# A low-bit test of the square weights, moved from the last units to the kernel's first microseconds

## The chip, the cores and the metric

The kernel runs on one core of a Trainium2 chip. A core has a matrix engine (TensorE, PE in the profile; its weight loads are listed as PEld), a vector engine (VectorE, DVE), a scalar engine (ScalarE, ACT), a general engine (GpSimd, POOL) and a queue processor (SyncE, SP). Each engine works through its own instructions in the order in which they were written, and waits on semaphores for the others. SyncE and ScalarE issue the transfers (DMA); SPq and ACTq are these issues in the profile. Data lies in HBM, in the on-chip memory SBUF (128 partitions), and in PSUM, where TensorE writes. The metric is device time in microseconds, from runs of the whole kernel.

## What is computed

The input x is 8 sequences of 512 positions with 128 features, in float32. A stack of six attention layers runs on the layer norm of x, and its result is added to x. A ternary feed-forward block runs on the layer norm of that, and is added again. Cut to what matters:

```python
def layer(h, p):                                   # six times
    q = (h @ wq.T + bq).reshape(bh, sl, 16, 8)
    k = (h @ wk.T + bk).reshape(bh, sl, 16, 8)
    scores = einsum('blhd,bmhd->bhlm', q, k) / sqrt(8)
    w_avg = softmax(scores).mean(axis=1)           # mean over 16 heads
    new_w = softmax(w_avg + rel)                   # rel: decay with distance
    h1 = ln(h + new_w @ h);  h2 = ln(h1)
    ff = relu(h2 @ w1.T + b1) @ w2.T + b2
    return ln(h2 + ff)

x = x + stack(layernorm(x))
v = layernorm(x)
h = silu((v @ w1.T) * s1) * ((v @ w2.T) * s2)      # 128 -> 512, weights -1, 0, 1
h = gelu((h @ h1.T) * t1);  h = gelu((h @ h2.T) * t2)   # 512 -> 512
x = x + (h @ w3.T) * s3
```

## The kernel before

**Units and steps.** A unit is one layer for one sequence: 6 x 8 = 48 units, layer by layer (`units`, line 222). A unit has 32 steps (`PAIRS`). A step makes two score tiles of 128 rows by 512 keys: 32 query positions for four heads in one matmul (line 451). For each tile VectorE takes the negated row maximum (`top`, line 462) and ScalarE the exponential with its row sum (`e`, line 471). A group is two steps; eight steps make one block of 128 positions (`lc`), and four blocks a unit.

**Stacks.** The score matmuls run on stacked operands. `project_k` and `project_q` multiply the transposed input hT by the layer's `wqk`; ScalarE writes kT and qT with their biases (lines 257 and 266, the biases from `bk_col` and from `bqs`, which VectorE scales out of `bq_col` in line 710). VectorE cuts each into a high part with the low twelve bits cleared (`hik`, `hiq`, line 274), GpSimd forms the remainder (`lok`, `loq`, line 275) and spreads the query parts under a head mask (`m0`, `m1`, line 311). Transfers then stack them: `stack_k` (16 of them into `ks`), `stack_q` (16 for half a unit into `qs`). In the first unit `stack_first` builds the first half in 32 smaller ones, and ScalarE issues a part of these and of `stack_k`. The pool for `qs` has two buffers. Two of the first unit's masks stand in buffers of the `e` pool, which are needed again for its third group.

**The order of the work** is written by hand. `at(step, place, fn)` puts a piece of work at a place within a step; steps are counted from the first unit's start, those before it from -64 on. In the prologue the first sequence's norm stands at steps -55 to -35, the transpose of its result at -33, `bqs` at -32, its projections at -28 and -27, `split_k` at -26, `split_q` at -24, the masks and `stack_first` at -14 and -13. The second sequence's norm stands at -12 to -3. `plan_before` and `plan_after` place a unit's preparation and its end (norms, MLP) into the steps of its neighbours; `sum_rows`, a GpSimd addition of two rows of the layer's parameters, is at step 3 of a layer's first unit. Between the engines the order of issue of the transfers is found by the program's builder, and each transfer signals its end on one of a few semaphores, which are used in turn.

**Loads at the start.** SyncE loads x of sequences 0 and 1 (256 KB each), then `load_layer(0)`: wqk (128 KB), w1, w2 (256 KB each) and `rows` (448 KB: seven parameter rows, copied to all partitions). ScalarE issues nine small loads of columns (line 125), behind three activations over the decay table and ahead of its copy of hT (line 250). In the code, the column loads stand between the loads of x and `load_layer(0)`. Later layers are loaded in the same order from unit 4 of the layer before.

**The low-bit test.** The block at the end has two arms. `gated_split` uses a faster matmul form that asks for weights whose low twelve bits are zero; `gated` is the general one. To choose, the kernel looks at the ten square weight blocks (fw1, fw2, and four blocks each of fh1 and fh2, 128 x 512): `load_square(k)` brings a block from HBM into a staging tile `square` (pool tag `x`) and copies it from there to its place; `low_bits(k)` keeps the low bits with an AND on VectorE (line 157) and takes their maximum (line 160). This is spread over units 41 to 45, two blocks a unit, the loads at steps 1 and 16, the tests at 7 and 23. `low_bits_row` reduces the ten maxima to one column (line 164) and sends it by a transfer into one row, in the last unit's step 7; `low_bits_end` reduces the row (line 168) in step 23. After the last unit, all engines read the number and take one arm (line 939).

Of the kernel before, what the change touches and what calls it, by code (L numbers as in the profile page):

```python
# [9 lines left out]
F32 = mybir.dt.float32  # L10
F32R = mybir.dt.float32r
I32 = mybir.dt.int32
# [5 lines left out]
P = 128  # L18
# [11 lines left out]
def attn_stack_then_ffn(ctx: ExitStack, tc: tile.TileContext, a: dict, out: bass.AP):  # L30
# [65 lines left out]
        nc.sync.dma_start(t, x[b].rearrange("(c p) e -> p c e", p=P))  # L96
        return t

    for b in range(2):
        x_in[b] = load_x(b, f"in{b}")  # L100
    lay = {}

    def load_layer(d):
        qk = wts.tile([P, 2, E], F32, tag="wqk", name=f"wqk_{d}", bufs=2)
        nc.sync.dma_start(qk, a["wqk"][d].rearrange("t e o -> e t o"))
        w1 = wts.tile([P, F], F32, tag="w1", name=f"w1_{d}", bufs=2)
        nc.sync.dma_start(w1, a["w1t"][d])
        w2 = wts.tile([P, FC, E], F32, tag="w2", name=f"w2_{d}", bufs=2)
        nc.sync.dma_start(w2, a["w2t"][d].rearrange("(c p) e -> p c e", p=P))
        r = wts.tile([P, len(ROWS), E], F32, tag="rows", name=f"rows_{d}", bufs=2)  # L110
        nc.sync.dma_start(
            r.rearrange("p k e -> p (k e)"),
            a["rows"][d].rearrange("k e -> (k e)").partition_broadcast(P),
        )
        rows = {name: r[:, k, :] for k, name in enumerate(ROWS)}
        lay[d] = (qk, w1, w2, rows)

    cols = {}
    for name, shape in (
# [3 lines left out]
    ):  # L123
        cols[name] = wts.tile(shape, F32, tag=name, name=name)
        nc.scalar.dma_start(cols[name], a[name])
    load_layer(0)

    fw1 = wts.tile([P, HID], F32, name="fw1")
    fw2 = wts.tile([P, HID], F32, name="fw2")
    fh1 = wts.tile([P, HC, HID], F32, name="fh1")  # L130
# [8 lines left out]
    low = state.tile([P, 2 + 2 * HC], I32, name="low")  # L139
    low_row = state.tile([1, P], I32, name="low_row")  # L140
    low_any = state.tile([1, 1], I32, name="low_any")

    staged = {}

    def load_square(k):

        name, c = ("f_w1t", "f_w2t", "f_h1t", "f_h2t")[k if k < 2 else 2 + (k - 2) // HC], (k - 2) % HC
        t = staged[k] = state.tile([P, HID], F32, tag="x", name=f"square_{k}", bufs=3)
        nc.sync.dma_start(t, a[name] if k < 2 else a[name][c * P : (c + 1) * P, :])
        nc.sync.dma_start(  # L150
            (fw1, fw2)[k] if k < 2 else (fh1, fh2)[(k - 2) // HC][:, c, :], t
        )

    def low_bits(k):

        t = staged.pop(k)
        nc.vector.tensor_scalar(
            t.bitcast(I32), t.bitcast(I32), ~LOW12, None, ALU.bitwise_and
        )
        nc.vector.tensor_reduce(low[:, k : k + 1], t.bitcast(I32), AX.X, ALU.max)  # L160

    def low_bits_row():
        most = state.tile([P, 1], I32, name="low_most")
# [3 lines left out]
    def low_bits_end():  # L167
        nc.vector.tensor_reduce(low_any, low_row, AX.X, ALU.max)

    bqs = wts.tile([P, D], F32, name="bqs")  # L170


# [60 lines left out]
    class Unit:  # L233
# [18 lines left out]
        def project_k(self):  # L252
            d = self.d
            pk = ring([P, L], f"pk_{self.n}")
            self.kT = work.tile([P, L], F32, tag="kT", name=f"kT_{self.n}", bufs=1)
            nc.tensor.matmul(pk, lay[d][0][:, 1, :], self.hT, start=True, stop=True)
            return lambda: nc.scalar.activation(  # L257
                self.kT, pk, AF.Identity, bias=cols["bk_col"][:, d : d + 1]
            )

        def project_q(self):
            d = self.d
            pq = ring([P, L], f"pq_{self.n}")
            self.qT = work.tile([P, L], F32, tag="qT", name=f"qT_{self.n}", bufs=1)
            nc.tensor.matmul(pq, lay[d][0][:, 0, :], self.hT, start=True, stop=True)
# [79 lines left out]

        def sum_rows(self):

            rows = lay[self.d][3]
# [4 lines left out]
            self.ln = Norm(self.z1, self.z1, f"a{self.n}")  # L353

        def affine_a(self, k):
            rows = lay[self.d][3]
# [7 lines left out]
            self.ln = Norm(self.z1, self.v, f"b{self.n}")  # L364

        def affine_b(self, k):
            rows = lay[self.d][3]
# [13 lines left out]
            )  # L381

        def hidden(self, f):
            w1 = lay[self.d][1]
            if f == 0:
                self.g = work.tile([P, FC, L], F32, tag="g", name=f"g_{self.n}", bufs=1)
            pf = ring([P, L], f"pf_{self.n}_{f}")
            nc.tensor.matmul(pf, w1[:, f * P : (f + 1) * P], self.uT, start=True, stop=True)  # L388
            k = self.d * FC + f
            def relu():  # L390
                if f == 1:
                    nc.vector.tensor_scalar(
                        self.g[:, f, :], pf, cols["b1_col"][:, k : k + 1], 0.0, ALU.add, ALU.max
                    )
                else:
                    nc.scalar.activation(
                        self.g[:, f, :], pf, AF.Relu, bias=cols["b1_col"][:, k : k + 1]
                    )

            return relu  # L400

        def mlp_out(self, half):
            w2 = lay[self.d][2]
# [14 lines left out]
            self.ln = Norm(self.z3, self.z3, f"c{self.n}")  # L418

        def affine_c(self, k):  # L420
            rows = lay[self.d][3]
# [281 lines left out]
    def plan_before(un):  # L703

        t = un.u * PAIRS
        if un.d == 0:
            first_steps = (20, 21, 26, 28, 29) if un.u == 1 else (9, 14, 26, 28, 29)
            norm_steps(t - 2 * PAIRS, un, un.norm_in, *first_steps)
        if un.u == 0:
            at(-PAIRS, D2, lambda: nc.vector.tensor_scalar_mul(bqs, cols["bq_col"], ISD))  # L710
        s = t - PAIRS
        matmuls(s, (5, P1, 5, A0), un.project_k)
        matmuls(s, (4, P0, 5, A1), un.project_q)
        at(s + 6, D2, un.split_k)
# [298 lines left out]
```

## Time and profile before

| | |
|---|---|
| median of three runs | 2647.22 us (2646.22 to 2648.22) |
| profiled execution, its own time | 2649.35 us |
| its span in the profile | 2647.4 us |
| granted TensorE clock over the span | 0.994 |
| first exponential of the first unit (ACT, line 471) | at 26.8 us |
| one unit in the middle of the kernel | 49.6 us |
| line 392, one instruction a unit: its 38th and its 45th start | 1989.28 and 2348.18 us |
| DMA traffic | 273.66 MB, of which 13.86 MB read from HBM |

All times in the profile count from the span's start and come from one execution; the times of runs are of executions without a profile. A line of the groups gives line, engine, operation, output and inputs, count and durations; a line of the timeline gives start, duration, engine and line; a line of the chain gives start, duration and what the end of the kernel waited for then. "Landing" is the time from the issue of a transfer to its completion.

### The profile page before, as it was taken

To read this page: it belongs to the slowest core of one execution; us is meant where nothing else is said; L and a number is where in the kernel's file an instruction comes from. 1 tells how busy PE (TensorE), PEld (TensorE's weight loads), DVE (VectorE), ACT (ScalarE), POOL (GpSimd) and SP (SyncE) were. 2 spreads that over 40 slices of the span, in tenths; PEclk is the share of its full clock that TensorE was granted. 3 is DMA by queue.
4 is the path that set the end of the run, shared out by engine and by line. 5 is a ranking of instruction groups with operands and counts; after the bars stand their busy time and mean duration, and the time that the engine had idled before them with its cause. 6 is when DMAs were issued, how large, how long until landed. Compare 5 with 4: busy or idle time off the path is not lost.

```text
span 2647.4 us, 50361 instructions
## 1 busy us (share of the span) xinstructions
PE 2559.2 (97%) x14944; PEld 1437.8 (54%) x14944; DVE 2489.0 (94%) x5773; ACT 2459.8 (93%) x6798; POOL 1812.5 (68%) x1894
## 2 busy tenths in 40 slices
PE   6999999999999999999999999999999999998999
PEld 2455555555555555555555555555555555555787
DVE  5999999999999999999999999999999999998774
ACT  6999999999999999999999999999999999997443
POOL 4667777677677677677677677677677667675874
PEclk8999999999999999999999999999999999999999
DMA  6445444455444444444445454455444545541000
GB/s 144 107 115 124 104 113 103 104 114 119 105 112 103 105 113 120 105 114 102 105 111 122 104 114 102 104 114 120 104 112 110 127 119 122 130 95 41 9 25 17
DMA packets 135846, 273.66 MB, mean 103 GB/s; under 512 B 39696, under 2 KB 57232, under 8 KB 135568
## 3 DMA queue, kind: packets, MB, share of 16 engines
q1 hardware_dynamic: 133504, 269.31, 43.8%
q8 instruction: 121, 1.98, 0.3%
q10 hardware_dynamic: 2064, 1.08, 0.2%
q14 instruction: 157, 1.29, 0.2%
HBM read 13.86 MB, written 2.10 MB: 6 GB/s over the span
## 4 chain that ended last, share of the span: by engine, by line
ACT 36%; DVE 32%; PE 26%; issue 3%; POOL 1%; DMA 1%; SPq 1%; ACTq 0%; POOLq 0%; DVEq 0%
ACT e L471 31%; DVE top L462 24%; PE acc L493 9%; PE ps L451 6%; PE qh L579 4%; DVE wT L511 2%; PE po L519 1%; PE pf L388 1%; ACT w L501 1%; ACT uT L378 1%; DVE z L415 1%; PE fo L625 1%; ACT kT L257 1%; PE pt_w L213 1%; PE q L579 1%
## 5 line engine op out<-in xcount | busy, mean ns | idle before, releaser
L471 ACT ACTIVATE e<-ps,top 128x512 f32<-128x512 f32 x3072 | 2092.5, 735 | 54.7 <-DVE top L462 29.2
L462 DVE TENSOR_REDUCE top<-ps 128x1 f32<-128x512 f32 x3072 | 1921.2, 679 | 60.5 <-PE ps L451 54.4
L451 PE MATMUL ps<-ks,qs 128*128 128x512 f32 x3040 | 1155.8, 469 | 27.7 <-ACT e L471 19.5
L451 PEld LDWEIGHTS ps<-ks,qs 128*128 128x128 f32 x3040 | 531.7, 188 | 666.0 <-ACT e L471 419.8
L471 ACT ACTIVATION_READ_ACCUMULATOR e<-ps,top 128x1 f32 x3072 | 780.6, 254 | 0.0
L493 PE MATMUL acc<-e,rp 128*32 128x512 f32 x6144 | 740.4, 600 | 0.8 <-POOL rp L482 0.8
L493 PEld LDWEIGHTS acc<-e,rp 128*32 128x32 f32 x6144 | 160.4, 109 | 331.2 <-issue 328.0
L482 POOL TENSOR_TENSOR rp<-pick,r 128x256 f32<-128x256 f32 x384 | 237.4, 618 | 133.8 <-DVE r L480 93.4
L311 POOL TENSOR_TENSOR m<-hiq,mask 128x512 f32<-128x512 f32 x190 | 242.2, 1286 | 0.7 <-DMA qs_first<-m_first 0.7
L311 POOL TENSOR_TENSOR m<-loq,mask 128x512 f32<-128x512 f32 x190 | 241.4, 1283 | 0.0
L519 PEld LDWEIGHTS po<-h,wT 128*128 128x128 f32 x1536 | 202.0, 192 | 17.3
L519 PE MATMUL po<-h,wT 128*128 128x129 f32 x1536 | 203.3, 275 | 0.0
L388 PE MATMUL pf<-uT,w 128*128 128x512 f32 x384 | 196.6, 593 | 3.7 <-ACT e L471 1.7
L408 PEld LDWEIGHTS py<-w,g 128*128 128x128 f32 x1536 | 182.6, 191 | 23.4 <-ACT e L471 19.1
L408 PE MATMUL py<-w,g 128*128 128x128 f32 x1536 | 191.7, 278 | 0.0
L197 POOL TENSOR_TENSOR rs_c<-mv_c,eps 128x4 f32<-128x4 f32 x48 | 9.7, 202 | 248.0 <-DVE r L480 228.3
L213 PE MATMUL pt_w<-ident,w 128*128 128x128 f32 x768 | 120.8, 280 | 17.7 <-ACT e L471 7.8
L275 POOL TENSOR_TENSOR lok<-kT,hik 128x512 f32<-128x512 f32 x48 | 61.5, 1280 | 101.6 <-DVE hik L274 101.6
L511 DVE TENSOR_TENSOR wT<-pt_w,decay 128x512 f32<-128x512 f32 x192 | 129.8, 676 | 0.1
L501 ACT ACTIVATE w<-acc 128x512 f32<-128x512 f32 x192 | 123.2, 642 | 0.0
L213 PEld LDWEIGHTS pt_w<-ident,w 128*128 128x128 f32 x768 | 86.4, 141 | 59.0 <-ACT e L471 45.2
L275 POOL TENSOR_TENSOR loq<-qT,hiq 128x512 f32<-128x512 f32 x48 | 61.4, 1279 | 76.6 <-DVE hiq L274 76.6
(116 smaller groups left out, 2665.8 us busy)
## 6 DMA issues: line engine op xcount, KB each, us to landing
qs<-m SPq DMA_DIRECT2D x1520, 128.0 KB, 2.4
ks<-hik SPq DMA_DIRECT2D x384, 64.0 KB, 2.0
ks<-lok SPq DMA_DIRECT2D x376, 64.0 KB, 2.0
rows<-in_rows SPq DMA_DIRECT2D x6, 448.0 KB, 5.1
x_in<-in_x SPq DMA_DIRECT2D x8, 256.0 KB, 3.0
fh<-square SPq DMA_DIRECT2D x8, 256.0 KB, 2.3
x_out<-in_x SPq DMA_DIRECT2D x8, 256.0 KB, 2.9
out<-y SPq DMA_DIRECT2D x7, 256.0 KB, 2.4
```

The source lines that it names most:

```text
L213: nc.tensor.transpose(pt[:, c * P : (c + 1) * P], src[:, c, :], ident)
L311: nc.gpsimd.tensor_tensor(m[:, lc - 2 * two], part.unsqueeze(2).to_broadcast([P, NB, PER_STRIP, QB]), mask.unsqueeze(1).to_broadcast([P, N ...
L388: nc.tensor.matmul(pf, w1[:, f * P : (f + 1) * P], self.uT, start=True, stop=True)
L408: nc.tensor.matmul(self.py[:, k, :], self.g[:, f, c * P : (c + 1) * P], w2[:, f, :], start=(f == 0), stop=(f == FC - 1),)
L451: nc.tensor.matmul(ps[s], qs[:, nb * P : (nb + 1) * P].bitcast(F32R), un.ks[:, i, :].bitcast(F32R), start=True, stop=True,)
L462: nc.vector.tensor_reduce(top[s], ps[s], AX.X, ALU.max, negate=True)
L471: nc.scalar.activation(self.e[:, nb, :], ps[s], AF.Exp, bias=top[s], accum_out=self.zs[:, i % 2, nb : nb + 1],)
L482: nc.gpsimd.tensor_tensor(self.rp.rearrange("p t n l -> p (t n) l"), pick.unsqueeze(1).to_broadcast([P, 2 * NB, QB]), r.rearrange("p t n - ...
L493: nc.tensor.matmul(acc[nb * QB : (nb + 1) * QB, :], self.rp[:, gr.turn % 2, nb, :], gr.e[:, nb, :], start=(gr.turn == 0), stop=(gr.turn == ...
L501: nc.scalar.activation(self.w.rearrange("p c l -> p (c l)"), acc, AF.Exp, scale=1.0 / H)
L511: nc.vector.tensor_tensor(self.wT.rearrange("p c l -> p (c l)"), self.pt, decay[:, LC - 1 - lc : 2 * LC - 1 - lc, :].rearrange("p c l -> p ...
L519: nc.tensor.matmul(self.po, self.wT[:, c, :], self.unit.h[:, c, 0 : E + 1], start=(c == 0), stop=(c == LC - 1),)
```

## The change

`load_layer` is split. `load_qk(d)` loads wqk alone; for layer 0 it stands between the loads of the two first sequences. The rest of layer 0 (w1, w2, rows) is loaded at the beginning of unit 0's loop body, on SyncE behind the stacks of the first half unit and the load of sequence 2. `sum_rows` of the first unit moves from step 3 to step 12.

`look_at_square` loads all ten square blocks from HBM at the start, behind x of sequence 1, two blocks to a part: the first part into the buffer of tag `g` (the MLP's hidden tile, first needed for the first unit in unit 2), the other four into one buffer of tag `qs` (16 KB a partition), which is the one that the first unit's second half takes. `low_bits(part)` now tests two blocks, 1024 columns, with the same two instructions: parts 0 and 1 at steps -31 and -30, parts 2, 3 and 4 at step -5, `low_bits_row` at step -4 and `low_bits_end` at the second unit's first step. `load_square` stays where it was, with both of its transfers, and no test follows it.

```diff
-    for b in range(2):
-        x_in[b] = load_x(b, f"in{b}")
+    def load_qk(d):
+        lay_qk[d] = wts.tile([P, 2, E], F32, tag="wqk", name=f"wqk_{d}", bufs=2)
+        nc.sync.dma_start(lay_qk[d], a["wqk"][d].rearrange("t e o -> e t o"))
...
     def load_layer(d):
-        qk = wts.tile([P, 2, E], F32, tag="wqk", name=f"wqk_{d}", bufs=2)
-        nc.sync.dma_start(qk, a["wqk"][d].rearrange("t e o -> e t o"))
...
+    x_in[0] = load_x(0, "in0")
+    load_qk(0)
+    x_in[1] = load_x(1, "in1")
...
-    load_layer(0)
...
+    def look_at_square():
+
+        first = work.tile([P, 2, HID], F32, tag="g", name="look_first", bufs=1)
+        rest = proj.tile([P, 2 * HC, HID], F32, tag="qs", name="look_rest")
+        for part in range(1 + HC):
+            looked[part] = first if part == 0 else rest[:, 2 * part - 2 : 2 * part, :]
+            for k in range(2):
+                nc.sync.dma_start(looked[part][:, k, :], square_block(2 * part + k)[0])
 
     def load_square(k):
 
-        name, c = ("f_w1t", "f_w2t", "f_h1t", "f_h2t")[k if k < 2 else 2 + (k - 2) // HC], (k - 2) % HC
-        t = staged[k] = state.tile([P, HID], F32, tag="x", name=f"square_{k}", bufs=3)
-        nc.sync.dma_start(t, a[name] if k < 2 else a[name][c * P : (c + 1) * P, :])
...
-    def low_bits(k):
-
-        t = staged.pop(k)
-        nc.vector.tensor_scalar(
-            t.bitcast(I32), t.bitcast(I32), ~LOW12, None, ALU.bitwise_and
-        )
-        nc.vector.tensor_reduce(low[:, k : k + 1], t.bitcast(I32), AX.X, ALU.max)
+        src, dst = square_block(k)
+        t = state.tile([P, HID], F32, tag="x", name=f"square_{k}", bufs=3)
+        nc.sync.dma_start(t, src)
+        nc.sync.dma_start(dst, t)
+
+    def low_bits(part):
+
+        t = looked.pop(part).bitcast(I32)
+        nc.vector.tensor_scalar(t, t, ~LOW12, None, ALU.bitwise_and)
+        nc.vector.tensor_reduce(low[:, part : part + 1], t, AX.XY, ALU.max)
...
+    look_at_square()
     bqs = wts.tile([P, D], F32, name="bqs")
...
-            at(t + 3, D2, un.sum_rows)
+            at(t + (12 if un.u == 0 else 3), D2, un.sum_rows)
...
+    for k, step in enumerate((-31, -30, -5, -5, -5)):
+        at(step, D2, lambda k=k: low_bits(k))
+    at(-4, D2, low_bits_row)
+    at(PAIRS, D2, low_bits_end)
...
-        at((U - 7 + k // 2) * PAIRS + (7, 23)[k % 2], D2, lambda k=k: low_bits(k))
-    at((U - 1) * PAIRS + 7, D2, low_bits_row)
-    at((U - 1) * PAIRS + 23, D2, low_bits_end)
...
         if un.b == 4 and un.d + 1 < D:
+            load_qk(un.d + 1)
             load_layer(un.d + 1)
+        if u == 0:
+            load_layer(0)
```

More of the change, by code (lines that the diff above doesn't have):

```diff
@@ L97, in load_x @@
         return t
-    for b in range(2):
-        x_in[b] = load_x(b, f"in{b}")
-    lay = {}
+    lay_qk, lay = {}, {}
+    def load_qk(d):
+        lay_qk[d] = wts.tile([P, 2, E], F32, tag="wqk", name=f"wqk_{d}", bufs=2)
+        nc.sync.dma_start(lay_qk[d], a["wqk"][d].rearrange("t e o -> e t o"))
     def load_layer(d):
-        qk = wts.tile([P, 2, E], F32, tag="wqk", name=f"wqk_{d}", bufs=2)
-        nc.sync.dma_start(qk, a["wqk"][d].rearrange("t e o -> e t o"))
         w1 = wts.tile([P, F], F32, tag="w1", name=f"w1_{d}", bufs=2)
@@ L114, in load_layer @@
         )
-        rows = {name: r[:, k, :] for k, name in enumerate(ROWS)}
-        lay[d] = (qk, w1, w2, rows)
+        lay[d] = w1, w2, {name: r[:, k, :] for k, name in enumerate(ROWS)}
+    x_in[0] = load_x(0, "in0")
+    load_qk(0)
+    x_in[1] = load_x(1, "in1")
     cols = {}
@@ L137, in load_ffn, with square_block @@
         nc.sync.dma_start(fw3s, a["f_w3s"].partition_broadcast(P))
-    low = state.tile([P, 2 + 2 * HC], I32, name="low")
+    low = state.tile([P, 1 + HC], I32, name="low")
     low_row = state.tile([1, P], I32, name="low_row")
     low_any = state.tile([1, 1], I32, name="low_any")
-    staged = {}
-    def load_square(k):
-        name, c = ("f_w1t", "f_w2t", "f_h1t", "f_h2t")[k if k < 2 else 2 + (k - 2) // HC], (k - 2) % HC
-        t = staged[k] = state.tile([P, HID], F32, tag="x", name=f"square_{k}", bufs=3)
-        nc.sync.dma_start(t, a[name] if k < 2 else a[name][c * P : (c + 1) * P, :])
-        nc.sync.dma_start(
-            (fw1, fw2)[k] if k < 2 else (fh1, fh2)[(k - 2) // HC][:, c, :], t
-        )
-    def low_bits(k):
-        t = staged.pop(k)
-        nc.vector.tensor_scalar(
-            t.bitcast(I32), t.bitcast(I32), ~LOW12, None, ALU.bitwise_and
-        )
-        nc.vector.tensor_reduce(low[:, k : k + 1], t.bitcast(I32), AX.X, ALU.max)
+    looked = {}
+    def square_block(k):
+        if k < 2:
+            return a[("f_w1t", "f_w2t")[k]], (fw1, fw2)[k]
+        c = (k - 2) % HC
+        name, t = (("f_h1t", fh1), ("f_h2t", fh2))[(k - 2) // HC]
+        return a[name][c * P : (c + 1) * P, :], t[:, c, :]
+    def look_at_square():
[5 more added lines that the diff above has]
+                nc.sync.dma_start(looked[part][:, k, :], square_block(2 * part + k)[0])
+    def load_square(k):
+        src, dst = square_block(k)
[6 more added lines that the diff above has]
+        nc.vector.tensor_reduce(low[:, part : part + 1], t, AX.XY, ALU.max)
     def low_bits_row():
@@ L255, in project_k @@
             self.kT = work.tile([P, L], F32, tag="kT", name=f"kT_{self.n}", bufs=1)
-            nc.tensor.matmul(pk, lay[d][0][:, 1, :], self.hT, start=True, stop=True)
+            nc.tensor.matmul(pk, lay_qk[d][:, 1, :], self.hT, start=True, stop=True)
             return lambda: nc.scalar.activation(
@@ L264, in project_q @@
             self.qT = work.tile([P, L], F32, tag="qT", name=f"qT_{self.n}", bufs=1)
-            nc.tensor.matmul(pq, lay[d][0][:, 0, :], self.hT, start=True, stop=True)
+            nc.tensor.matmul(pq, lay_qk[d][:, 0, :], self.hT, start=True, stop=True)
             return lambda: nc.scalar.activation(
@@ L346, in sum_rows @@
         def sum_rows(self):
-            rows = lay[self.d][3]
+            rows = lay[self.d][2]
             rows["b2s"] = wts.tile([P, E], F32, tag="b2s", name=f"b2s_{self.d}", bufs=2)
@@ L355, in affine_a @@
         def affine_a(self, k):
-            rows = lay[self.d][3]
+            rows = lay[self.d][2]
             if k == 0:
@@ L366, in affine_b @@
         def affine_b(self, k):
-            rows = lay[self.d][3]
+            rows = lay[self.d][2]
             if k == 0:
@@ L383, in hidden @@
         def hidden(self, f):
-            w1 = lay[self.d][1]
+            w1 = lay[self.d][0]
             if f == 0:
@@ L402, in mlp_out @@
         def mlp_out(self, half):
-            w2 = lay[self.d][2]
+            w2 = lay[self.d][1]
             self.py = ring([P, 2, E], f"py_{self.n}_{half}")
@@ L420, in affine_c @@
         def affine_c(self, k):
-            rows = lay[self.d][3]
+            rows = lay[self.d][2]
             if k == 0:
```

## The prediction

> **What bounds the kernel now.** I read the page first, then the groups of one tile, a timeline of VectorE (DVE), busy times by window, and last the chain of waits at the kernel's start. The page's first part:
>
> ```profile
> PE 2559.2 (97%) x14944; PEld 1437.8 (54%) x14944; DVE 2489.0 (94%) x5773; ACT 2459.8 (93%) x6798; POOL 1812.5 (68%) x1894
> ```
>
> Three engines above 90%: whatever keeps one of them may show one for one. The tile that stages a square weight block has these VectorE groups (duration minimum, median, maximum in ns; first and last start in us):
>
> ```profile
> L157 DVE TENSOR_SCALAR square<-square x10: 417/470/535, 2078.2 to 2312.0; 128x512 int32<-128x512 int32 x10
> L160 DVE TENSOR_REDUCE low<-square x10: 685/686/689, 2078.7 to 2312.5; 128x1 int32<-128x512 int32 x10
> ```
>
> They occupy 10 x (0.470 + 0.686) = 11.56 us of VectorE between 2078 and 2313. What that costs is read off an instruction that runs once a unit, the VectorE relu of line 392, in the timeline (start, duration):
>
> ```profile
> 1989.28 0.74 DVE L392 TENSOR_SCALAR g<-pf,b_col 128x512 f32<-128x512 f32 x1
> ...
> 2038.89 0.75 DVE L392 TENSOR_SCALAR g<-pf,b_col 128x512 f32<-128x512 f32 x1
> ...
> 2348.18 0.74 DVE L392 TENSOR_SCALAR g<-pf,b_col 128x512 f32<-128x512 f32 x1
> ```
>
> A clean unit takes 2038.89 - 1989.28 = 49.61 us. The next six, which hold all ten tests, take 309.29 us, or 11.6 more than six clean ones. Busy times of a clean window and of one unit with two tests (window, length; PE, PEld, DVE, ACT, POOL; clock, DMA share, GB/s):
>
> ```profile
> 1000.00:1050.00 50.00, 49.34 (x300) 26.66 (x292) 48.88 (x115) 49.53 (x142) 34.98 (x37) 1.00 0.53 128
> 2141.50:2193.60 52.10, 50.54 (x294) 26.73 (x293) 50.71 (x119) 49.53 (x140) 34.62 (x37) 1.00 0.51 124
> ```
>
> The reader should see ACT: 0.47 us idle in the first window, 2.57 in the second. ScalarE bounds the clean unit; during a test it runs out of row maxima. So the tests stand on the path in full. Now the start, by the chain of waits:
>
> ```profile
> 3.32 5.36 DMA rows<-in_rows
> 8.69 0.33 ACTq L125
> 9.07 0.45 ACTq L125
> 9.55 0.59 ACT hT L250
> 10.19 2.07 PE pq L265 x2
> 12.27 1.47 PE pk L256 x2
> 13.76 0.70 ACT kT L257
> 14.48 0.44 DVE hik L274
> ...
> 33.85 2.04 DMA qs_first<-m_first
> 36.07 0.63 ACT e L471
> ```
>
> The first copy on ScalarE, hT, stands behind ScalarE's nine column loads, and the last two of these were held by the landing of `rows`. The issues just before show the rule, beside the landing times of SyncE's last loads (us from issue, last column):
>
> ```profile
> 6.73 0.33 ACTq L125 DMA_DIRECT2D f_w1s_col<-in_f_w1s_col  x1
> 7.56 0.33 ACTq L125 DMA_DIRECT2D f_w2s_col<-in_f_w2s_col  x1
> ```
>
> ```profile
> rows<-in_rows SPq DMA_DIRECT2D x1, 448.0 KB, 5.4
> w<-in_w1t SPq DMA_DIRECT2D x1, 256.0 KB, 4.4
> w<-in_w2t SPq DMA_DIRECT2D x1, 256.0 KB, 4.7
> ```
>
> w1, issued at 2.32, lands at 6.72; w2, issued at 2.84, at 7.54; rows, issued at 3.32, at 8.69. At just these moments f_w1s, f_w2s and f_h1s go out. Counting issues (SyncE's six: x0, x1, wqk, w1, w2, rows; then ScalarE's nine), w1 is fourth and f_w1s twelfth: an issue waits until the transfer eight places earlier has landed.
>
> **The change, part by part.**
>
> *Tests leave the units* (`low_bits` at steps 7 and 23): ten pairs go, -11.6 us by the six units. The other measure, VectorE's busy time, gives 11.56; I take 11.6, with 10 as the lower end, should the `load_square` waits on SyncE, which stay, carry some of it. `low_bits_row` (one 0.15 us reduction) leaves unit U-1 too, -0.15; `low_bits_end` (0.26 us) only changes its unit, 0.
>
> *Ten loads of 256 KB enter SyncE's queue at the start; w1, w2, rows leave it.* Ahead of both groups stand the same 640 KB (x0, x1, wqk in another order), so the first square load should land where w1 did, at 6.7 us. From w1's landing to that of rows, 704 KB took 1.97 us, 366 GB/s; each further 256 KB adds 0.72 us, and the tenth lands at 6.7 + 9 x 0.72 = 13.2. By w2's gap alone (0.82 us per 256 KB) it is 14.1, by that of rows (1.15 us per 448 KB) 12.6. SyncE itself takes about 0.5 us an issue, thirteen by 8 us; its last two wait for the first square loads, at 6.7 and 7.4 us, with over 1 MB still under way, so nothing runs dry.
>
> *What waits for them.* By the count above, f_h1s becomes the twenty-first issue and waits for the thirteenth, the tenth square load; f_h2s waits for bq, the fourteenth. Behind them on ScalarE's queue stand hT, kT, qT and half of the stack copies; PE's pq waits for hT, VectorE's hik for kT, both stack queues for hik. From rows' landing to hT it was 0.86 us; now 13.2 + 0.86 = 14.1 against 9.55: **+4.5 us** (3.9 to 5.4). PE's transposes for hT end at 9.35, so the whole delay shows. From hik to the e of 36.07 the chain is queue issues and their landing, and from 36 to 85 us ScalarE is busy 47.64 of 49.00: the delay reaches the end one for one.
>
> *Two tests in front of hik* (steps -31, -30, behind bqs). bq landed at 8.86, 0.17 after rows, though issued at 4.18; I take 0.17 after the tenth load, 13.4. A test now covers 1024 columns, at most twice the old pair, 2.3 us, and not under 1.8 if a quarter of it is fixed cost. They end at 17.2 to 18.2; hik is due at 14.48 + 4.5 = 19.0. Cost 0, hidden by the two projections on PE; without that cover up to 4.6.
>
> *Three tests at step -5*, behind unit 1's statistics, which end at 17.6 + 4.5 = 22.1: 5.4 to 6.9 us, and longer beside POOL's masks (hiq took 1.47 us beside POOL's lok, hik 0.43 alone: up to 1.04 more for each). They end at 27.5 to 32.1; the first row maximum is due at 25.39 + 4.5 = 29.9. Up to 2.2 late, covered by the 3.33 us that ScalarE idles before 36.07 for an e buffer. POOL may lose a VectorE operation (at most 1.07) now and then: ScalarE's queue takes the second mask 1.4 us after it is ready and SyncE its third about 5 after, so 0 to 0.7; I take 0. If both covers went: up to 2.9.
>
> *SyncE in unit 0.* The low_row issue (0.54), w1, w2 and rows (0.47, 0.43, 0.50) now precede sixteen stack copies: 1.9 us later, and 960 KB at 366 GB/s are 2.7 us of transfer. The thirteenth copy (issued near 44.0, landing 2.4 to 2.9 later) completes the first strip that the matmul at 52.08 reads; 5.2 us of cover against 4.6. Cost 0, at worst 1. `sum_rows` at step 12 lies on POOL between the rp at 43.01 and that at 49.94; rows should be in at about 43.3, all on the old clock. The looked-at buffers: the g slot is first used in unit 2, the stack slot at 36, both after the tests.
>
> *Sum*: -11.6 - 0.15 + 4.5 = -7.3 us. The profiled execution took 2649.35 (span 2647.4 and 1.95 around it), so it would take 2642.1; it stands 2.13 above the median of the runs, 2647.22, from which I forecast **2639.9 us**.
>
> One rule speaks against the change. The Trainium skill, "DMA: Bandwidth & Descriptors", section "Anatomy of one DMA", gives each DMA about 2.0 us plus its bytes over 436 GB/s (fitted on another issue path). Taken one after another, ten loads of 256 KB would be an estimated 26 us against 8 for the three that leave, and the sum +6. The rows above speak for overlap, landing 0.8 and 1.15 us apart.
>
> **Rivals.**
>
> *A, column loads not behind the square loads.* If the order of issues puts ScalarE's nine ahead of most square loads, hT stays near 9.6. For it: on ScalarE they are ready at 4.18, when SyncE has issued some seven loads. Against it: before, all six loads of SyncE were counted first, though four stand behind the columns in the code. Time: 2647.2 - 11.75 = 2635.5.
>
> *B, a later start.* The tests show in front of hik (bqs more than 1 us late), or the bulk runs at 200 GB/s rather than 366: 1600 KB more at the head cost 8.2 us instead of 4.5. For it: the slowest 0.3 us of the old burst moved 176 GB/s. Against: w1, w2 and rows. Time: 2647.2 - 11.75 + 8.5 = 2644.
>
> *C, slower: the loads run one after another.* A square load alone took 2.9 us to land; ten in series are 29 us, less the three removed in the same way (2.9 + 2.9 + 5.1): +18.1 at hT, 2653.6. It decides above 17 us of delay, where the 1600 KB more move at 96 GB/s. Against it: about 300 GB/s over the first loads, with six issued before the second landed.
>
> *D, the tests were free.* Refuted by the six units unless SyncE's waits made their 11.6 us; it would give about 2651.
>
> **How the numbers follow.** Forecast 0.60 (own range 2638.5 to 2642), A 0.14, B 0.19, C 0.04, D 0.03. A measurement here tells about 0.2%, 5.3 us, from no change. Below 2641.9: A and nearly all of the forecast's case, 0.71. Within: the rest of it and B, 0.22. Above 2652.5: C, part of D, 0.07 with what I don't see. The range 2635 to 2645 holds the forecast's case, A and most of B, and leaves out C and D.
>
> **What would show it.** Right: line 392 at 49.6 us intervals up to 2348 on the old clock; f_h1s issued when the tenth square load lands, near 13.2; hT near 14.1; hik near 19 with ScalarE's kT, not a test, ending just before; e after its buffer wait near 40.5; no wait on a stack transfer at step 16 of unit 0. Wrong: hT near 9.6 (A); hik behind a test or a load landing after 15 (B), after 25 (C); intervals that stay at 51 to 52 (D).

## The result, and the profile after

| | before | after |
|---|---|---|
| median of 22 runs each, side by side | 2646.28 us (2644.52 to 2648.74) | 2642.08 us (2640.22 to 2645.67) |
| profiled execution: time, span | 2649.35, 2647.4 us | 2644.57, 2642.7 us |
| the once-a-unit instruction: 1st, 38th, 45th start | 149.23, 1989.28, 2348.18 us | 156.21, 1995.84, 2343.55 us |

The ratio is 0.9985, with a 95% interval of 0.9980 to 0.9991: 4.2 us faster, or 0.15%. That lies within the stated range and inside the band that the prediction called no change; the forecast had been 7.3 us, a chance of 0.71 for more than 0.2%, and 0.22 for a result within it. The profiled executions differ by 4.8 us.

The first line of the page of after differs little from the one of before: ScalarE is busy 0.7 us less, VectorE 1.0, TensorE 7.4. The shares hardly move; the rest has to be read by place.

```profile
PE 2551.8 (97%) x14944; PEld 1436.8 (54%) x14944; DVE 2488.0 (94%) x5763; ACT 2459.1 (93%) x6798; POOL 1815.6 (69%) x1894
```

The relu that runs once a unit (line 392, now 407) divides the kernel into places. Its first, 38th, 39th and 45th start in VectorE's timeline of after (start, duration):

```profile
156.21 0.74 DVE L407 TENSOR_SCALAR g<-pf,b_col 128x512 f32<-128x512 f32 x1
...
1995.84 0.74 DVE L407 TENSOR_SCALAR g<-pf,b_col 128x512 f32<-128x512 f32 x1
...
2045.45 0.73 DVE L407 TENSOR_SCALAR g<-pf,b_col 128x512 f32<-128x512 f32 x1
...
2343.55 0.74 DVE L407 TENSOR_SCALAR g<-pf,b_col 128x512 f32<-128x512 f32 x1
```

Its first start in before:

```profile
149.23 0.74 DVE L392 TENSOR_SCALAR g<-pf,b_col 128x512 f32<-128x512 f32 x1
```

So after is 6.98 us behind by the first relu and 6.56 behind at the 38th. From the 39th to the 45th it takes 2343.55 - 2045.45 = 298.10 us for six units where before took 309.29, and is then 4.63 us ahead. The gain in the units is 11.19 us, near the forecast of 11.6. The loss ahead of the first relu is 6.98, not 4.5, and there the difference lies.

The chain of waits at the start of after (start, duration, what was waited for):

```profile
2.28 3.97 DMA look_first<-in_f_w1t
...
6.26 6.19 DMA look_rest<-in_f_h2t
...
12.48 1.61 DMA f_w2s_col<-in_f_w2s_col
...
14.09 0.59 ACT hT L265
```

Square loads and column loads now stand where `rows` and the last two column issues stood. The timeline of all engines adds the instructions that the prediction had named:

```profile
13.22 0.33 ACTq L128 DMA_DIRECT2D f_h1s_col<-in_f_h1s_col  x1
...
13.40 0.17 DVE L725 TENSOR_SCALAR bqs<-bq_col 128x6 f32<-128x6 f32 x1 [8.66 <-DMA bq_col<-in_bq_col]
13.49 0.69 DVE L173 TENSOR_SCALAR look_first<-look_first 128x1024 int32<-128x1024 int32 x1
...
18.87 0.43 DVE L289 TENSOR_SCALAR hik<-kT 128x512 int32<-128x512 int32 x1 [1.58 <-ACT kT L272]
...
40.72 0.69 ACT L486 ACTIVATE e<-ps,top 128x512 f32<-128x512 f32 x1 [3.59 <-DMA qs_first<-m_first]
```

f_h1s goes out at 13.22 (forecast 13.2), hT runs at 14.09 (14.1), `hik` waits 1.58 us for ScalarE's kT and not for a test, and the e behind the buffer wait starts at 40.72 against 36.07. The start is 4.65 us later, 0.15 from what was worked out. The remaining 6.98 - 4.65 = 2.33 us are lost between 41 and 156 us. TensorE's timeline shows where (what stands in brackets is the idle time before, and what ended it), in before and then in after:

```profile
52.08 0.49 PE L451 MATMUL ps<-ks,qs 128*128 128x512 f32 x1
...
53.19 1.93 PE L493 MATMUL acc<-e,rp 128*32 128x512 f32 x16
55.04 0.96 PE L451 MATMUL ps<-ks,qs 128*128 128x512 f32 x3
```

```profile
58.05 0.75 PE L466 MATMUL ps<-ks,qs 128*128 128x512 f32 x2 [1.47 <-DMA qs<-m]
58.73 3.50 PE L508 MATMUL acc<-e,rp 128*32 128x512 f32 x16
62.16 0.96 PE L466 MATMUL ps<-ks,qs 128*128 128x512 f32 x3
```

TensorE waits 1.47 us for the second half's stack (`qs`), and the sixteen small matmuls behind the wait (called the gather below), which the neighbouring groups do in 1.92 us, take 3.50. Behind them after is 62.16 - 55.04 = 7.12 us late, so the whole 2.33 us is lost here. SyncE's part of it in after (start, time over all of the group):

```profile
41.60 0.50 SPq L107 DMA_DIRECT2D w<-in_w1t  x1
42.14 0.43 SPq L109 DMA_DIRECT2D w<-in_w2t  x1
42.62 0.50 SPq L111 DMA_DIRECT2D rows<-in_rows  x1
43.22 12.48 SPq L342 DMA_DIRECT2D qs<-m  x16
```

and the sixteen copies in before:

```profile
36.44 10.04 SPq L327 DMA_DIRECT2D qs<-m  x16
```

The copies take 2.4 us longer to issue. The landing time of the second half's stack tile (minimum, median, maximum over its sixteen copies) was, in before and then in after:

```profile
DMA to landing us min/median/max: 3.4/3.8/3.9
```

```profile
DMA to landing us min/median/max: 4.2/4.7/7.5
```

The chain of after in this stretch ties a late issue to a long landing:

```profile
45.73 7.45 DMA qs<-m
...
53.20 4.71 DMA qs<-m
...
58.05 0.75 PE ps L466 x2
```

The fifth copy, issued at 45.73, took 7.45 us. As it lands, at 53.18, the next issue in the chain goes out, as an issue does that waits for the one eight places earlier: the thirteenth, the very one that completes the strip TensorE reads. At 0.63 us a copy, the pace of before, it would have gone out near 43.22 + 12 x 0.63 = 50.8, 2.4 us earlier; then it took 4.71 to land. Where SyncE lost the 2.4 us is seen from its own waits in this stretch (who waits, for what; us in total, times, longest):

```profile
SPq L342 <- DMA rows<-in_rows: 1.8, 1, 1.8
SPq L342 <- DMA w<-in_w2t: 0.7, 1, 0.7
```

These are the eighth and the seventh copy, which stand eight places behind `rows` and w2. So layer 0's loads held the copies in SyncE's queue, and from the ninth to the fourteenth each goes out as the one eight places earlier lands. The busy times (window, length; PE, PEld, DVE, ACT, POOL; clock, DMA share, GB/s) of before in the stretch around the gather, and then of after:

```profile
50.00:56.00 6.00, 4.99 (x29) 2.23 (x29) 6.00 (x13) 6.00 (x20) 0.77 (x2) 1.00 0.38 91
56.00:62.00 6.00, 5.83 (x36) 2.95 (x34) 5.96 (x13) 6.00 (x20) 4.95 (x6) 1.00 0.48 111
```

```profile
50.00:56.00 6.00, 4.80 (x25) 1.74 (x25) 6.00 (x14) 5.81 (x18) 1.07 (x2) 1.00 0.98 208
56.00:62.00 6.00, 4.53 (x22) 1.23 (x22) 4.11 (x10) 5.09 (x15) 1.72 (x2) 0.72 0.53 124
```

In after the transfer engines are busy 0.98 of the first window; in the second VectorE has 1.9 us and ScalarE 0.9 us of idle time, at a granted TensorE clock of 0.72 (1.00 is full speed).

### The profile page after: what moved, and what is told of

Read it like the earlier page. It is cut to its first block, busy times and chain, and to the rows that moved or that the text cites. A ratio compares the mean times of both kernels' runs of the same rounds, so it can differ in the third digit from the quotient of the medians.

```text
span 2642.7 us, 50377 instructions
## 1 busy us (share of the span) xinstructions
PE 2551.8 (97%) x14944; PEld 1436.8 (54%) x14944; DVE 2488.0 (94%) x5763; ACT 2459.1 (93%) x6798; POOL 1815.6 (69%) x1894
## 3 DMA queue, kind: packets, MB, share of 16 engines
q10 hardware_dynamic: 2064, 1.08, 0.2%
## 4 chain that ended last, share of the span: by engine, by line
ACT 36%; DVE 30%; PE 26%; issue 3%; POOL 2%; DMA 1%; SPq 1%; DVEq 0%; POOLq 0%; ACTq 0%
ACT e L486 31%; DVE top L477 22%; PE acc L508 10%; PE ps L466 7%; PE qh L594 4%; PE po L534 1%; PE pf L403 1%; DVE wT L526 1%; ACT w L516 1%; ACT uT L393 1%; DVE z L430 1%; ACT kT L272 1%; PE pt_w L228 1%; PE fo L640 1%; ACT g L411 1%
```

## The experiments

Theory 1: the missing gain is layer 0's w1, w2 and rows (960 KB), which share the transfer engines with the second half's stack copies. Theory 2: the 4.5 us at the start are ScalarE's nine column issues held behind ten square loads, and the bulk itself costs nothing. Rivals: the tests beside GpSimd cost unit 0 the 2.3 us; or something in the last units returned part of the gain. In the readings below "the start" is the first exponential behind the buffer wait against 36.07, and "unit 0" is what the first relu, against 149.23, loses beyond it.

**Layer 0's loads 22 steps later.** Against after:

```diff
-            at(t + (12 if un.u == 0 else 3), D2, un.sum_rows)
+            at(t + (44 if un.u == 0 else 3), D2, un.sum_rows)
...
+    at(22, D2, lambda: load_layer(0))
...
-        if u == 0:
-            load_layer(0)
```

> The changed kernel, with w1, w2 and rows of layer 0 loaded at step 22 of unit 0, behind the stacks, where SyncE was idle, and their sum at step 44. Theory 1 (the 960 KB stood in the way of the second half's stack copies, whose transfers had filled the DMA engines before): the first matmul on the second stack no longer waits for a transfer, line 407 stands 4.6 to 4.9 us behind its old place in unit 2 instead of 6.98, and the time is 2.3 us under that of the changed kernel, about 2639.8. Rival (unit 0 is late because of what the tests did to VectorE and GpSimd before it): the matmul still waits, line 407 stays near +7, and the time stays at 2642.

Measured: 2640.07 us (2638.65 to 2641.77), ratio to before 0.9975 (0.9966 to 0.9985); before read 2646.89 beside it. The first relu starts at 153.96, the start is at 41.02: +4.95, and unit 0 -0.2. TensorE's timeline has no wait for a transfer, and the gather is back:

```profile
56.87 0.51 PE L466 MATMUL ps<-ks,qs 128*128 128x512 f32 x1
...
57.97 1.92 PE L508 MATMUL acc<-e,rp 128*32 128x512 f32 x16
```

SyncE's copies no longer wait for a load of layer 0. The five tests stand where they stood, so it is the loads, not the tests, that cost unit 0 its 2.3 us.

**The loads moved, and nothing else.** Against before, with wqk between the two loads of x as in the change, and no square load or test moved:

```diff
-    load_layer(0)
...
-            at(t + 3, D2, un.sum_rows)
+            at(t + (12 if un.u == 0 else 3), D2, un.sum_rows)
...
+            load_qk(un.d + 1)
             load_layer(un.d + 1)
+        if u == 0:
+            load_layer(0)
```

> The kernel before, with only the move of w1, w2 and rows of layer 0 into unit 0 (and wqk ahead of the second x); tests as before. Theory 1: the copy of hT is bounded by TensorE's transposes at 9.35 us, so the start gains at most 0.2 us, and the stack copies collide in unit 0: line 392 in unit 2 about 2 us later than 149.23, the time about 2 us above before. Rival (the collision needs the late start or the low-bit transfer): no change, within 0.3 us. A third reading, that the shorter burst at the start is worth more than 0.2 us, would show hT under 9.3 us.

Measured: 2649.43 us (2646.33 to 2654.14), ratio 1.0010 (1.0001 to 1.0020): slower than before by 2.5 us. The start gains nothing (e at 35.91), the first relu is at 151.06, +1.83. The same picture stands in TensorE's timeline, without a late start and without tests:

```profile
52.89 0.70 PE L453 MATMUL ps<-ks,qs 128*128 128x512 f32 x2 [1.08 <-DMA ks<-hik]
53.52 3.31 PE L495 MATMUL acc<-e,rp 128*32 128x512 f32 x16
```

**The column loads ahead of the square loads.** Against after:

```diff
-        nc.scalar.dma_start(cols[name], a[name])
+        nc.sync.dma_start(cols[name], a[name])
```

> The changed kernel, with the nine column loads on SyncE ahead of the ten square loads, none on ScalarE. Theory 2 (the start was late only because ScalarE's issues waited for the transfers eight places earlier, the square loads): hT near 9.5 us, the first e after the buffer wait near 36.3 us instead of 40.72, and the time about 4.4 us under the changed kernel, 2637.7, though the square loads end later, near 15 us. Rival (the bytes themselves delay the start, by the stack copies or by the two tests in front of hik): hik above 16 us and less than half of the 4.4 us gained.

Measured: 2638.83 us (2635.74 to 2638.93), ratio 0.9971 (0.9960 to 0.9982). From the timeline:

```profile
9.64 0.58 ACT L265 COPY hT<-pt_h 128x512 f32<-128x512 f32 x1 [4.52 <-PE pt_h L228]
...
14.81 0.43 DVE L289 TENSOR_SCALAR hik<-kT 128x512 int32<-128x512 int32 x1 [0.65 <-ACT kT L272]
...
53.58 1.19 PE L466 MATMUL ps<-ks,qs 128*128 128x512 f32 x2 [1.83 <-DMA qs<-m]
```

hT is back at 9.64 and waits for TensorE's transposes, when nine of the ten square loads have not landed. The start is +0.44; the first relu, at 151.52, still shows the loss in unit 0. One word of the code, which puts nine small loads into SyncE's queue ahead of the square loads, is worth 4.2 us at the start (4.65 - 0.44).

**No test at all.** Against before; the low-bit test is left out, and the arm is chosen by a constant zero:

```diff
-        at((U - 7 + k // 2) * PAIRS + (7, 23)[k % 2], D2, lambda k=k: low_bits(k))
-    at((U - 1) * PAIRS + 7, D2, low_bits_row)
-    at((U - 1) * PAIRS + 23, D2, low_bits_end)
+    nc.vector.memset(low_any, 0)
```

> The kernel before, without the ten tests, their row and its end: the number that chooses the arm is set to 0, so the low-bit test of the weights is left out; the loads of the square weights stay as they were. Theory 3 (the tests cost their VectorE time, one for one): units of 49.6 us throughout, 11.6 us under before, 2634.7. Rival (part of the 11.6 us was the wait of SyncE between the two transfers of a square load): units 41 to 46 stay above 49.9 us and the gain is under 10 us.

Measured: 2634.83 us (2634.09 to 2636.24), ratio 0.9956 (0.9943 to 0.9970), 12.1 us less than before beside it. The six units take 2336.53 - 2038.53 = 298.00 us, 11.29 less than in before. The `load_square` waits are all still in SyncE's queue, so this was the tests' VectorE time (11.56), nearly in full. One thing more: the start of this kernel is the code of before, yet its first exponential behind the buffer wait stands at 36.82, 0.75 us later than there, and its first relu at 150.03. Its loads landed that much later (the first column load that is held for one goes out at 7.52, against 6.73). So differences under about 0.8 us at the start of single executions tell nothing, here and below.

**Both mends together.** Column loads first, and layer 0's loads at step 22; against after:

```diff
-        nc.scalar.dma_start(cols[name], a[name])
+        nc.sync.dma_start(cols[name], a[name])
...
-            at(t + (12 if un.u == 0 else 3), D2, un.sum_rows)
+            at(t + (44 if un.u == 0 else 3), D2, un.sum_rows)
...
+    at(22, D2, lambda: load_layer(0))
...
-        if u == 0:
-            load_layer(0)
```

> The changed kernel with both edits: column loads on SyncE ahead of the square loads, and w1, w2, rows of layer 0 at step 22 of unit 0. If the two losses are separate and are all that the start cost: hT near 9.6 us, e after its buffer wait near 36.3, no wait for a stack transfer at step 16, line 407 in unit 2 at 149.2 to 149.6 as in the kernel before, and a time 11.6 us under before, about 2635, as without any test. If something else of the change costs (the tests beside GpSimd, the longer SyncE queue): line 407 above 150.2 or above 2636.5.

Measured: 2635.26 us (2634.34 to 2635.38) beside 2647.57 for before, ratio 0.9953 (0.9939 to 0.9966). From the timeline:

```profile
9.66 0.58 ACT L265 COPY hT<-pt_h 128x512 f32<-128x512 f32 x1 [4.55 <-PE pt_h L228]
...
36.68 0.69 ACT L486 ACTIVATE e<-ps,top 128x512 f32<-128x512 f32 x1 [3.52 <-DMA qs_first<-m_first]
```

The first relu is at 149.71, 0.48 behind before and 0.32 ahead of the kernel without a test. This version beats both kernels, and can't be told from the kernel without a test: what five tests and ten more loads at the start cost is within what the start differs by between executions.

**Half of every square block.** Against after; the right half of each block is neither loaded at the start nor tested:

```diff
...
-                nc.sync.dma_start(looked[part][:, k, :], square_block(2 * part + k)[0])
+                nc.sync.dma_start(looked[part][:, k, :], square_block(2 * part + k)[0][:, : HID // 2])
```

> The changed kernel, with the left half of each square block looked at only (ten loads of 128 KB, tests of half the width), so half of the test is left out. If hT waits for the bytes of the tenth load at 366 GB/s: the tenth lands near 6.4 + 9 x 0.36 = 9.6 us and hT starts near 10.5, against 14.09. If it waits for the number of issues (ten more of some 0.5 us) or for a fixed latency of each load, hT stays above 12.

Measured: 2640.51 us in one execution. From the timeline:

```profile
7.20 0.39 ACTq L128 DMA_DIRECT2D bq_col<-in_bq_col  x1
...
11.52 0.59 ACT L265 COPY hT<-pt_h 128x512 f32<-128x512 f32 x1 [6.39 <-DMA f_w2s_col<-in_f_w2s_col]
```

hT came 2.6 us earlier with half the bytes, but 1.0 later than expected. The first column load, still held for the load eight places earlier, now goes out at 7.20; behind it ScalarE needs 4.3 us for its nine issues, about 0.48 each, back to back. At half the bytes the issues have become the limit, and I had not counted them. (The two tiles are cut to half as well.) In unit 0 this kernel lost only 0.4 us, although its loads stand where after has them: TensorE's wait for the stack was 0.79 us, and the gather stayed at 1.92, at a clock of 1.00.

**Four columns fewer on ScalarE.** Against after; the four columns of the feed-forward block are loaded by SyncE much later:

```diff
-        nc.scalar.dma_start(cols[name], a[name])
+        if not name.startswith("f_"):
+            nc.scalar.dma_start(cols[name], a[name])
...
     def load_ffn():
+        for name in ("f_w1s_col", "f_w2s_col", "f_h1s_col", "f_h2s_col"):
+            nc.sync.dma_start(cols[name], a[name])
```

> The changed kernel with the four column loads of the feed-forward block moved to SyncE at its later weight load; five stay on ScalarE. If an issue waits for the transfer eight places earlier, the last one (ln2b, the eighteenth) waits for the tenth, the seventh square load, which lands near 11.1 us: hT near 11.6 instead of 14.09, while the square loads still end near 13.2. bq then still lands near 13.3, so the two tests end near 17.3 and hold hik (kT is ready near 16.4): hik near 17.4, and e after its buffer wait near 39.2. If hT waits for the whole burst, it stays near 14.

Measured: 2642.45 us in one execution. hT at 11.82 is as expected (11.6), and the test now stands in front of `hik`, as the timeline shows:

```profile
16.34 1.22 DVE L177 TENSOR_REDUCE low<-look_rest 128x1 int32<-128x1024 int32 x1
...
17.48 0.42 DVE L292 TENSOR_SCALAR hik<-kT 128x512 int32<-128x512 int32 x1
```

The start is at 39.80 (expected 39.2). But the first relu is at 156.53, as late as in after: unit 0 lost 3.57 us here, and the 0.92 us won at the start was gone. Two more runs asked whether that was the collision again.

**The same four columns, without the collision.** The last edit and the first one together, against after:

```diff
-        nc.scalar.dma_start(cols[name], a[name])
+        if not name.startswith("f_"):
+            nc.scalar.dma_start(cols[name], a[name])
...
+        for name in ("f_w1s_col", "f_w2s_col", "f_h1s_col", "f_h2s_col"):
+            nc.sync.dma_start(cols[name], a[name])
...
-            at(t + (12 if un.u == 0 else 3), D2, un.sum_rows)
+            at(t + (44 if un.u == 0 else 3), D2, un.sum_rows)
...
+    at(22, D2, lambda: load_layer(0))
...
-        if u == 0:
-            load_layer(0)
```

> The kernel after, with both the four f_ columns in SyncE's later load and layer 0's w1, w2 and rows at step 22. In the run with the columns alone the start was 2.3 us earlier (hT 11.82) and unit 0 gave it back. Theory: unit 0 gave it back because the loads shared the time of the stack copies. Then without them the gain shows: hT near 11.8, the first exponential after its buffer wait near 39 to 40, no wait of TensorE for a transfer in unit 0, the gather at 1.92 us, the once-a-unit instruction 151.7 to 152.6 and a time of 2640.1 - 2 = 2638 us (2637 to 2639). Rival: the earlier start is lost for a reason of its own (the order of tests and split, or later column issues); then the once-a-unit instruction stays near 154 and the time near 2640.

Measured: 2639.66 us (2637.82 to 2640.01), with before at 2649.83 beside it; ratio 0.9958 (0.9941 to 0.9975). The start is at 39.13, +3.06; the first relu is at 152.50, so unit 0 lost 0.2. From TensorE's timeline:

```profile
55.80 0.50 PE L469 MATMUL ps<-ks,qs 128*128 128x512 f32 x1 [0.17 <-ACT e L489]
56.23 1.92 PE L511 MATMUL acc<-e,rp 128*32 128x512 f32 x16
```

The readings in the trace are those expected; without the loads the earlier start reaches the first relu. The time missed its band by 0.7 us, on a chip where before itself read 3 us more than beside the first runs.

**The four columns again, timed.** The edit is that of the kernel with four columns fewer, unchanged:

```diff
-        nc.scalar.dma_start(cols[name], a[name])
+        if not name.startswith("f_"):
+            nc.scalar.dma_start(cols[name], a[name])
...
```

> The same edit as the run with the four f_ columns in SyncE's later load, now timed in rounds beside other runs of the kernel before. Theory 1: that the 2.3 us at the start came to nothing there belongs to that edit, because the rows land at the same absolute time; then the time is that of the kernel after, 2642 (2641 to 2643). Theory 2: it was one execution's chance; then 2639.5 to 2640.5.

Measured: 2641.35 us (2639.80 to 2646.06), ratio 0.9972 (0.9961 to 0.9983), beside the same 2649.83. By the time alone this is the kernel after (2642.08), by the ratio it is 3 us better than it; the two readings can't be reconciled from these runs, so theory 1 against 2 stays open there. The profiled execution has a start of 38.68, against 39.80 in the first, and a first relu of 154.81: 1.4 earlier than after, with 2.97 us lost in unit 0. In both executions of this kernel unit 0 loses more than in after, in neither less. Beside the same before, the kernel without the collision took 1.7 us less, and its first relu stands 2.3 us earlier.

**Unit 0 over all kernels.** TensorE's idle time before its first matmul on the second half's stack, from the timelines of nine profiled executions, and the time for which SyncE held the stack copies for a load of layer 0:

| kernel | SyncE held, us | wait, us | gather behind it, us | lost in unit 0, us |
|---|---|---|---|---|
| loads at step 22 (three kernels) | 0 | 0.0 | 1.92 | -0.2 to 0.2 |
| half blocks | 1.9 | 0.79 | 1.92 | 0.4 |
| loads moved alone | 3.1 | 1.08 | 3.31 | 2.0 |
| after | 2.5 | 1.47 | 3.50 | 2.3 |
| columns first | 3.5 | 1.83 | 2.79 | 1.9 |
| four columns fewer, again | 2.9 | 1.78 | 3.38 | 3.0 |
| four columns fewer | 3.7 | 2.16 | 3.59 | 3.6 |

The end of the wait is put down to a stack copy in after, in columns first and in half blocks, to another stack's copy (`ks`) in the loads moved alone, and to an exponential in the last two rows. The landings settle these three: the thirteenth copy of `qs` landed 0.14 us before the matmul in the loads moved alone (52.75) and 0.09 before it in the last two (56.33, 58.01). Every kernel that has the loads ahead of the copies waits, and none of the others does. What the runs don't take apart is how much of it comes from the copies being issued late and how much from their sharing the transfer engines, as the loads were always moved as a whole.

## Why the prediction was right, and where it was wrong

*Tests leave the units, -11.6.* Right: -11.2 in the traces, and 12.1 us by time in the kernel without tests. Two of the six intervals of after are 49.83 and 49.88 where 49.61 is usual; the kernel without tests has such a pair at the same place, so they are not tests.

*The start, +4.5.* Right, +4.65, and for the reason given; that it came within 0.15 is luck, as one start differs by 0.75 us between executions. The landings of the square loads are stamped by the column issues that waited for them, some 0.7 us apart up to 13.22, near the 0.72 taken from w1 and rows. That an issue waits for the transfer eight places earlier, read off three issues of before, carried the whole of it, and putting the columns first removed it. Rival A's time, 2635.5, is what the two mends together give (2635.26), though nothing of A happened in the kernel after: the builder counted ScalarE's issues last, as before.

*Tests in front of hik, and beside GpSimd, 0.* Right. A test of 1024 columns took 0.69 + 1.22 = 1.91 us, within the 1.8 to 2.3 given, and beside GpSimd the AND took up to 1.72, the reduction 1.22 as before; the last of them ended at 29.84, and the first row maximum started at 29.95. The cover in front of `hik` was 1.58 us. It was real but thin: with hT 2.3 us earlier the second test does end just before `hik`.

*SyncE in unit 0, "cost 0, at worst 1".* This is the step that failed: 2.33 us. It put 4.6 us of delay against 5.2 us of cover, and both terms were mis-sized. The cover rested on a landing of 2.4 to 2.9 us for the thirteenth copy. In before it landed at 47.83, 3.85 after its issue at 43.98, which leaves 4.25 us to the matmul at 52.08. The delay, beyond the later start, was 5.43 us: the first copy went out 2.13 later (43.22 - 36.44 - 4.65; forecast 1.9), and in place of the 2.7 of transfer stand 2.44 more until the thirteenth issue and 0.86 more for its landing. That leaves 1.18 us uncovered, near the 1.47 that TensorE waited. The copies of before already took 3.8 us at the median, and its transfer view of the stretch from 36 to 53 us says why (busy share of the transfer engines in 40 slices, in tenths):

```profile
DMA  2519999999999999999999999999673363363265
```

The engines are full from 37 to 48 us, with sixteen copies of 128 KB as the greater part, so 960 KB more come on top of them and not beside them. Second, I used the rule of eight for the start and not here, where the seventh and eighth copies waited 2.5 us for w2 and `rows`, and the thirteenth for the fifth. Third, nothing in the sum stood for what came behind a wait: the gather took 1.58 us longer, at a lower clock, and a wait of 1.47 us became a loss of 2.33. With the term at 2.33 the sum is -11.2 + 4.65 + 2.33 = -4.2; the traces have -4.63 at the 45th relu, as between the first and the 38th after won back 0.42.

*The level.* The forecast stood on a median of three runs, 2647.22; 22 runs of before give 2646.28. The difference taken from these is 4.2 us, and the forecast's 2639.9 is 2.2 us below the measured time: 0.9 of the 3.1 us missing in the change were made up by the level. The result lies in the stated range of 2635 to 2645, and just outside the forecast's own, 2638.5 to 2642.

*The rule weighed there.* The Trainium skill, "DMA: Bandwidth & Descriptors", section "Anatomy of one DMA", taken serially would, by the prediction's estimate from its figures, have made the start some 18 us later. The trace has landings 0.7 us apart and +4.65; rival C did not happen. Nor did B, by its causes: the loads ran at the rate taken and no test showed. But its time, 2644, is as near to the result as mine, for another reason. D is refuted by the kernel without tests.

## What to carry to other kernels

A load that is moved off one busy stretch lands in another: before calling it hidden, read the landing time and the transfer share of the stretch it enters, and compare the bytes with what is spare there. When issues wait for the transfer a fixed number of places earlier, count every queue's issues in order, in the new place as well as the old; here nine small loads cost no more than 0.44 us ahead of the bulk ones, and behind them they held up the engine that issued them for 4.65. A wait of a microsecond on TensorE may be paid twice, once as the wait and once in slower work behind it.

## What the runs showed of the hardware

**A clock that falls behind a short wait.** In the table above, waits of up to 0.79 us are followed by a gather of 1.92 us, waits of 1.08 us and more by one of 2.79 to 3.59. The granted clock of the six microseconds around is 1.00 in the first cases and 0.72 in after; there, in windows of 2 us, it is 1.00 up to the matmul at 58.05, then 0.62 and 0.53, and 1.00 again. The Trainium skill, "TensorE: Matmul & The Clock Gate", section "Why this matters for your kernels", asks for no idle gap above about 3 us; here half of that went with a lower clock. That the wait, and not the thinner work around it, lowers the clock was not tried apart.

**Single executions differ behind the last unit, and the clock with them.** The relu's interval that holds the branch between the two arms was 70.00 us in before and 71.22 in after; in the other kernels, whose edits don't touch it, it lies between 68.18 and 71.23. Busy times (columns as above) of the two stretches of 5 us that begin 30 us into that interval, for before, for after, and for the kernel with both mends:

```profile
2427.62:2432.62 5.00, 3.31 (x13) 3.03 (x14) 1.95 (x4) 1.83 (x2) 2.03 (x4) 0.73 0.00 0
2432.62:2437.62 5.00, 5.00 (x28) 2.53 (x27) 3.49 (x7) 1.81 (x3) 1.36 (x2) 0.92 0.00 2
```

```profile
2422.97:2427.97 5.00, 3.31 (x11) 2.92 (x12) 1.70 (x3) 1.65 (x2) 1.64 (x2) 0.60 0.00 2
2427.97:2432.97 5.00, 5.00 (x26) 2.34 (x25) 3.08 (x7) 0.69 (x1) 2.28 (x2) 0.72 0.00 0
```

```profile
2415.75:2420.75 5.00, 3.35 (x20) 2.48 (x24) 2.78 (x4) 2.53 (x3) 2.17 (x4) 1.00 0.01 2
2420.75:2425.75 5.00, 3.71 (x25) 1.81 (x18) 4.16 (x9) 2.73 (x4) 2.40 (x3) 1.00 0.00 0
```

It is the second stretch that goes with the time, in all eleven executions: a clock of 0.71 or 0.72 there with 71.2 us (two kernels), 0.84 to 0.92 with 70.0 (three), and 0.99 or 1.00 with 68.2 to 68.4 (six). The first stretch does not decide: the kernel without a test has 0.66 there, 1.00 in the second, and 68.20 us. That the clock causes the difference was not tried apart. So three microseconds of a single execution, as much as was being looked for, lie in this place alone. The ends of two single profiles can mislead by as much: columns first ended 13.4 us ahead of before in the profile, where the runs differ by 8.1. A comparison place by place shows where the difference lies.
